# A graph-attention and hypergraph layer over 64 pairs of graphs: another order of the instructions in the software pipeline, and another plan for the preparation of the weights

## The chip, the cores and the metric

One core of one Trainium2 chip. The metric is the device time of the whole program in microseconds (us), as the median of several executions. The engines are called as the profile calls them: PE is TensorE, DVE is VectorE, ACT is ScalarE, POOL is GpSimd, SP is SyncE, which only issues DMA transfers here. I take each engine to work through its own instructions in the order of the program; in the profile of the kernel before, VectorE starts the same 87 instructions in the same order in 57 of the 63 stretches from the nodes of one pair to those of the next.

## The reference, cut to what matters

128 graphs of 128 nodes with 512 features each, fp32. Two layers, each with a residual and a normalisation behind it:

```python
# layer 0: graph attention, 8 heads of 64 features
feats   = einsum('bnf,hfu->bhnu', X, W)                # "pf" below
dense   = leaky_relu(e_self[:, None] + e_neigh[None])  # scores, 128 x 128 per head
dense   = dense + NEG_BIG * (1 - A)                    # mask
att     = softmax(dense)                               # exponentials e, sums
out     = relu(att @ feats + b)                        # "pav"
x       = layernorm(x + out)
# layer 1: two hypergraph convolutions, R = D^-1 H B^-1 H^T from the graph's adjacency
h = relu(R @ (x @ W1.T) + b1)                          # R first: "pz", then "ph"; 1024 wide
h = layer_norm(h) * gamma + beta
y = R @ (h @ W2.T) + b2                                # "py", then "pq"
x = layernorm(x + (y + x))
```

## The kernel before

The kernel takes two graphs (a pair) at a time. Each of the three large products (pf, ph, py) is computed as seven half-size products that gather in three PSUM banks X, Y and W, with sums of operands and of results on the other engines. These seven follow each other on TensorE, and the copies of bank X by ScalarE between them belong to the path:

```python
    def chain(kind, lag, times, multiply, w, extra=0):
        def product(p, s, i):
            where, start = {1: ("X", 1), 2: ("Y", 1), 6: ("X", 0), 5: ("W", 1), 7: ("X", 0),
                            4: ("X", 0), 3: ("W", 0)}[i]
            ...
        def copy(p, s, i):
            ...
            nc.scalar.copy(t[:, :n], s[kind, "X"][:, :n])
```

Every function of the pipeline is placed at a lag (in pairs) and a time within a pair. The order of these numbers is the order of the instructions on the engines; they are no waits. Those that the change moves:

```python
    @step(0, 32.7)
    def nodes(p, s):                 # node degrees of the next pair, on VectorE: seven small operations
        ...
            nc.vector.scalar_tensor_tensor(w[:, g, :], a[:, g, :], 0.0, w[:, g, :],
                op0=ALU.not_equal, op1=ALU.mult, accum_out=dd[:, g:g + 1])
        ...
        nc.vector.tensor_scalar(dn, dd, TINY, None, op0=ALU.max)
        ...
    for (g, q), tm, (lag, tl), (lagx, tx), te, tt in (
        ((0, 0), 32.7, (1, 33.4), (1, 34.8), 2.6, 18.1), ((0, 1), 34.0, (1, 35.7), (1, 37.3), 4.6, 18.15),
        ((1, 0), 35.2, (1, 37.9), (2, 2.0), 5.8, 20.0), ((1, 1), 36.4, (1, 39.0), (2, 2.7), 7.9, 20.7),
    ):
        at(1, tm, masked, g, q)         # GpSimd: scores + mask, one quarter of a pair
        at(lag, tl, leaky, g, q)        # ScalarE
        at(lagx, tx, largest, g, q)     # VectorE: maximum per row ("nm")
        at(2, te, exponential, g, q)    # ScalarE
        at(2, tt, e_transpose, g, q)    # VectorE, behind a trip of the exponentials through DRAM
    ...
    for (g, q), t in (((0, 0), 19.4), ((0, 1), 20.0), ((1, 0), 21.2), ((1, 1), 21.8)):
        at(3, t, square, g, q)          # ScalarE: h squared
    for g in range(2):
        for level in range(3):
            at(3, (25.4, 26.7, 27.4)[level] + 3.9 * g, squares, g, level)   # GpSimd: their sums
```

The weights are prepared within the first pairs. `once` lists this work by the pair in which it falls; `shift` moves one stretch of steps:

```python
    once = {
        0: [(11.0, prepare_first, ())],
        1: [(3.7, prepare_first_sums, ()), (26.3, prepare_hidden, ())],
        2: [(9.0, prepare_output, ()), (9.1, prepare_output_sums, ()),
            (41.5, prepare_output_blocks, (slice(0, 4),))],
        3: [(8.9, prepare_output_block_sums, ())],       # on GpSimd
    }
```

## Time and profile before

| | before |
|---|---|
| time, median | 2774.68 us (2773.65 to 2774.87; three executions, 2774.66 with a fourth) |
| first phX product of pair 0, of pair 1 | 99.80 us, 154.78 us |
| period, from pair 1 to pair 62 (61 pairs) | 41.59 us |
| from pair 62's first phX product to the end | 82.2 us |
| TensorE idle in front of pyW, pyX, phX, each time | 0.93, 0.45, 0.41 us |

I use the start of the first phX product (the first of the seven of ph) as the mark of a pair, since it stands once in each pair on TensorE. The idle times are those of the view of waits, which counts from the modelled end of the product before; the prediction counts from starts and adds the cost of restarting (about 0.1 us each after two of them: 1.83 us for 1.735 and 1.89 for 1.785), and so comes to 2.47 us per pair where these three come to 1.79.

The chain of work that ended last, by engine:

```profile
PE 37%; POOL 34%; DVE 14%; ACT 8%; issue 5%; DMA 1%; SPq 0%; POOLq 0%; DVEq 0%
```

TensorE is busy for 93% of the span, and still the path to the end runs through it for 37% only: in each pair the path leaves TensorE for GpSimd, VectorE and ScalarE and comes back at a hole. What the nodes cost on VectorE in the timeline (start, duration, instruction):

```profile
1019.34 0.28 DVE L305 SCALAR_TENSOR_TENSOR w<-a,w 128x128 f32<-128x128 f32 x1
...
1019.55 1.35 DVE L305 SCALAR_TENSOR_TENSOR w<-a,w 128x128 f32<-128x128 f32 x1
...
1020.94 1.12 DVE L310 TENSOR_SCALAR dn<-dd 128x2 f32<-128x2 f32 x1
```

The same operation on the same shape takes 0.28 and 1.35 us, and one on 128 by 2 elements takes 1.12 us. The long ones run beside the masks on GpSimd (three in a row, 1018.13 to 1022.03 us). Over the whole profile the one on 128 by 2 elements (dn) took 1.11 to 1.12 us in the 62 pairs in which it began while a mask ran, and 0.17 us in the two others.

### The profile page before, as it was taken

To read this page: it belongs to the slowest core of one execution; us is meant where nothing else is said; L and a number is where in the kernel's file an instruction comes from. 1 tells how busy PE (TensorE), PEld (TensorE's weight loads), DVE (VectorE), ACT (ScalarE), POOL (GpSimd) and SP (SyncE) were. 2 spreads that over 40 slices of the span, in tenths; PEclk is the share of its full clock that TensorE was granted. 3 is DMA by queue.
4 is the path that set the end of the run, shared out by engine and by line. 5 is a ranking of instruction groups with operands and counts; after the bars stand their busy time and mean duration, and the time that the engine had idled before them with its cause. 6 is when DMAs were issued, how large, how long until landed. Compare 5 with 4: busy or idle time off the path is not lost.

```text
span 2773.7 us, 48838 instructions
## 1 busy us (share of the span) xinstructions
PE 2576.7 (93%) x16608; PEld 2305.7 (83%) x16608; DVE 2049.4 (74%) x4584; ACT 1533.7 (55%) x4421; POOL 1785.0 (64%) x1813
## 2 busy tenths in 40 slices
PE   3599999999999999999999999999999999999997
PEld 2588888888888888888888888888888888888886
DVE  4577777777777777777777777777777777777764
ACT  2365565565565565565555555555565565555562
POOL 2566666666666666666666666666666666666664
PEclk9799999999999999999999999999999999999998
DMA  5444444444444444444444444444444444444430
GB/s 152 107 124 127 122 124 127 122 124 126 122 124 126 122 124 126 122 124 126 122 124 127 122 123 127 122 122 128 122 123 128 122 123 127 122 122 128 123 109 29
DMA packets 334348, 337.73 MB, mean 122 GB/s; under 512 B 99858, under 2 KB 266770, under 8 KB 334100
## 3 DMA queue, kind: packets, MB, share of 16 engines
q1 hardware_dynamic: 330404, 333.56, 42.6%
q8 instruction: 132, 2.16, 0.3%
q10 hardware_dynamic: 3696, 1.06, 0.2%
q14 instruction: 116, 0.95, 0.1%
HBM read 233.32 MB, written 101.19 MB: 121 GB/s over the span
## 4 chain that ended last, share of the span: by engine, by line
PE 37%; POOL 34%; DVE 14%; ACT 8%; issue 5%; DMA 1%; SPq 0%; POOLq 0%; DVEq 0%
PE phX L678 17%; POOL sq L729 12%; POOL hS L400 10%; PE phW L678 8%; POOL y L576 7%; PE phY L678 4%; PE pq L799 4%; DVE w L305 3%; ACT nb L492 3%; POOL nb L485 3%; ACT h L708 3%; DVE sh L614 3%; DVE dn L310 2%; PE pfX L418 2%; POOL rsa L599 2%
## 5 line engine op out<-in xcount | busy, mean ns | idle before, releaser
L492 ACT ACTIVATE nb<-nb,ft 128x128 f32<-128x128 f32 x1024 | 327.6, 395 | 285.4 <-POOL nb L485 206.0
L678 PEld LDWEIGHTS phX<-zS,w_sb 128*128 128x128 f32 x3072 | 366.2, 193 | 41.2 <-issue 30.4
L678 PE MATMUL phX<-zS,w_sb 128*128 128x128 f32 x3072 | 377.6, 276 | 10.5 <-POOL w_sb L257 7.9
L729 POOL TENSOR_TENSOR sq<-sq 128x512 f32<-128x512 f32 (+2 forms) x384 | 334.1, 870 | 20.1
L485 POOL TENSOR_TENSOR nb<-nb,neg 128x512 f32<-128x512 f32 x256 | 330.2, 1310 | 15.5 <-DMA nb<-rd 15.5
L289 ACT COPY py<-pyX 128x257 f32<-128x257 f32 (+1 forms) x192 | 70.3, 366 | 471.0 <-PE pyX L418 471.0
L506 ACT ACTIVATE nb<-nb,nm 128x128 f32<-128x128 f32 x1024 | 320.8, 394 | 1.8 <-DVE nm L498 1.8
L599 POOL TENSOR_TENSOR rso<-veo,mhalf 128x2 f32<-128x2 f32 x64 | 44.8, 700 | 406.4 <-DVE veo L597 406.4
L418 PE MATMUL pyW<-w_sb,hS 128*128 128x256 f32 x1024 | 249.7, 386 | 56.5 <-DVE y L761 56.5
L418 PE MATMUL pyX<-w_sb,h 128*128 128x257 f32 (+1 forms) x1024 | 251.6, 388 | 28.4 <-ACT py L289 28.1
L418 PEld LDWEIGHTS pyW<-w_sb,hS 128*128 128x128 f32 x1024 | 189.9, 190 | 105.8 <-DVE y L761 81.0
L708 ACT ACTIVATE h<-h,b_sb 128x128 f32<-128x128 f32 x768 | 244.6, 391 | 60.1 <-DVE h L693 60.1
L400 POOL TENSOR_TENSOR hS<-h 128x512 f32<-128x512 f32 x128 | 160.5, 1275 | 179.1 <-ACT h L708 179.1
L552 PEld LDWEIGHTS pav<-ft,eT 128*128 128x128 f32 x2048 | 252.8, 195 | 22.2 <-issue 11.6
L552 PE MATMUL pav<-ft,eT 128*128 128x65 f32 x2048 | 247.2, 275 | 13.4 <-DVE eT L527 13.4
L418 PE MATMUL pyX<-w_sb,hS 128*128 128x257 f32 (+1 forms) x1024 | 243.7, 380 | 2.5 <-POOL hS L400 2.5
L693 DVE TENSOR_TENSOR h<-ph,phW 128x512 f32<-128x512 f32 x128 | 88.0, 688 | 203.8 <-ACT ph L289 138.2
L418 PEld LDWEIGHTS pyX<-w_sb,h 128*128 128x128 f32 x1024 | 185.2, 191 | 55.2 <-ACT py L289 33.8
L418 PEld LDWEIGHTS pyX<-w_sb,hS 128*128 128x128 f32 x1024 | 194.0, 189 | 31.3 <-POOL hS L400 2.9
L576 POOL TENSOR_TENSOR y<-y,b_bc 128x512 f32<-128x512 f32 x128 | 190.4, 1487 | 30.8 <-DVE y L567 30.8
L527 DVE STREAM_TRANSPOSE eT<-eb 128x512 f32<-128x512 f32 x256 | 165.4, 685 | 10.6 <-DMA eb<-ed 10.6
L498 DVE TENSOR_REDUCE nm<-nb 128x4 f32<-128x512 f32 x256 | 168.4, 677 | 6.6 <-ACT nb L492 6.5
(125 smaller groups left out, 5843.5 us busy)
## 6 DMA issues: line engine op xcount, KB each, us to landing
nb<-rd SPq DMA_DIRECT2D x128, 512.0 KB
ed<-nb SPq DMA_DIRECT2D x128, 512.0 KB
eb<-ed SPq DMA_DIRECT2D x512, 128.0 KB
xb<-in_x_dram SPq DMA_DIRECT2D x256, 128.0 KB
x<-in_x_dram SPq DMA_DIRECT2D x64, 512.0 KB
out_dram<-o SPq DMA_DIRECT2D x64, 512.0 KB
a<-in_adj_dram SPq DMA_DIRECT2D x64, 128.0 KB
w<-in_adj_dram SPq DMA_DIRECT2D x128, 64.0 KB
```

Of the source, the lines that this page charges most:

```text
L400: engine.tensor_tensor(t[:, i], in0, in1, op=op)
L418: nc.tensor.matmul(to[:, :n], lhs[:, k, :], rhs[:, k, :n], start=bool(start) and k == 0, stop=(k == nk - 1), skip_group_check=True,)
L485: nc.gpsimd.tensor_tensor(t, t, neg[:, :, None, :].to_broadcast([P, NB, HH, B]), op=ALU.add)
L492: nc.scalar.activation(t, t, AF.Prelu, bias=s["ft"][:, g, h, 0:1], alpha=SLOPE)
L498: nc.vector.tensor_reduce(s["nm"][:, g, hs], scores(s, g, hs).rearrange("p b h j -> p h b j"), AX.XY, ALU.max, negate=True,)
L506: nc.scalar.activation(t, t, AF.Exp, bias=s["nm"][:, g, h:h + 1])
L527: nc.vector.transpose(s["eT"][:, g, hs, :].rearrange("p h (b i) -> p h b i", b=NB), s["eb", g][:, :, hs, :].rearrange("p b h j -> p h b j"),)
L552: nc.tensor.matmul(t[:, h * (U + 1):(h + 1) * (U + 1)], s["eT"][:, g, q * HH + h, :], s["ft"][:, g, q * HH + h, 2:], start=True, stop=True,)
L576: nc.gpsimd.tensor_tensor(s["y"][:, g, :], s["y"][:, g, :], b0_bc, op=ALU.add)
L678: nc.tensor.matmul(to[:, m * N:(m + 1) * N], w[:, k, m * P:(m + 1) * P], rhs[:, k, :], start=bool(start) and m == 0 and k == 0, stop=(k == ...
L708: nc.scalar.activation(dst[:, k, :], src[:, k, :], AF.Relu, bias=b1_sb[:, c:c + 1])
L729: nc.gpsimd.tensor_tensor(t[:, :n, :], t[:, :n, :], t[:, n:2 * n, :], op=ALU.add)
```

## The change

No arithmetic of the loop is added or removed. In the loop: the nodes go from the late place 32.7 to 11.0; masks, squares and their sums come earlier; the last leaky step goes behind the copies of zT; and the transpose of the score rows (pr), with which the load nb for the masks begins, comes half a pav earlier. In the preparation: one list of global times in place of the list by pairs, the third weight's sums on VectorE instead of GpSimd, the first weight in four transfers of rows by fours instead of sixteen by 32 (with a matching layout of the transposed x), and the first pair's exponentials transposed on TensorE instead of through DRAM. Cut to its core:

```diff
-    @step(0, 32.7)
+    @step(0, 11.0)
     def nodes(p, s):
...
-    @step(1, 25.95)
+    @step(1, 24.95)
     def transpose_scores(p, s):
...
-        ((0, 0), 32.7, (1, 33.4), (1, 34.8), 2.6, 18.1), ((0, 1), 34.0, (1, 35.7), (1, 37.3), 4.6, 18.15),
-        ((1, 0), 35.2, (1, 37.9), (2, 2.0), 5.8, 20.0), ((1, 1), 36.4, (1, 39.0), (2, 2.7), 7.9, 20.7),
+        ((0, 0), 31.0, (1, 32.5), (1, 34.8), 2.7, 18.1), ((0, 1), 33.0, (1, 35.4), (1, 37.3), 4.6, 18.15),
+        ((1, 0), 34.2, (1, 38.0), (2, 2.0), 7.8, 21.5), ((1, 1), 35.4, (2, 6.0), (2, 7.3), 7.9, 21.55),
...
-    at(3, 9.2, relu, 0, 0)
+    at(3, 11.5, relu, 0, 0)
-    for (g, q), t in (((0, 0), 19.4), ((0, 1), 20.0), ((1, 0), 21.2), ((1, 1), 21.8)):
+    for (g, q), t in (((0, 0), 13.5), ((0, 1), 15.9), ((1, 0), 19.4), ((1, 1), 21.2)):
         at(3, t, square, g, q)
-            at(3, (25.4, 26.7, 27.4)[level] + 3.9 * g, squares, g, level)
+            at(3, ((17.0, 17.1, 17.2), (26.0, 28.5, 28.6))[g][level], squares, g, level)
...
-        rows = w0.rearrange("(b k f) c -> b f k c", b=NB, k=KF)
-        for b in range(NB):
-            nc.sync.dma_start(raw[b * B:(b + 1) * B],
-                rows[b][:, i * KF // 2:(i + 1) * KF // 2, j * QU:(j + 1) * QU])
+        nc.sync.dma_start(raw, w0.rearrange("(p k) c -> p k c", k=KF)
+            [:, i * KF // 2:(i + 1) * KF // 2, j * QU:(j + 1) * QU])
...
-            s["xb"][:, g * NB:(g + 1) * NB].rearrange("p b (k f) -> p k b f", k=KF),
+            s["xb"][:, g * NB:(g + 1) * NB].rearrange("p b (f k) -> p k b f", k=KF),
...
+    def e_transpose_first(p, s):     # 16 nc.tensor.transpose, 4 nc.scalar.copy; pair 0 alone
...
-    once = { ... }
+    T = 39.2
+    todo = [
+        (11.1, prepare_first, (0,)), (12.0, prepare_first, (1,)), (13.0, prepare_first_sums, ()),
+        (65.0, prepare_output, ()), (71.4, prepare_output_sums, ()), (73.7, prepare_hidden, (0,)),
+        (75.6, prepare_hidden, (1,)), (77.5, prepare_hidden, (2,)), (77.6, prepare_hidden, (3,)),
+        (82.0, prepare_output_blocks, ()), (83.0, prepare_output_block_sums, ()),   # now on VectorE
+    ]
+    def shift(p, lag, time): ...     # moves some steps of pairs 0 and 1
+    for p in range(PAIRS):
+        ...
+            todo.append(((p + lag) * T + time + shift(p, lag, time), on_pair, (fn, p)))
+    todo.append((2 * T + 2.1, on_pair, (e_transpose_first, 0)))
```

More of the change, by code (lines that the diff above doesn't have):

```diff
@@ L130 @@
     w0_blocks = []
-    for dst, i, j in ((w0_sb[:, 0], 0, 0), (w0_12, 0, 1), (w0_sb[:, 1], 1, 0), (w0_sb[:, 2], 1, 1)):
+    for dst, i, j in ((w0_sb[:, 0], 0, 0), (w0_sb[:, 1], 1, 0), (w0_12, 0, 1), (w0_sb[:, 2], 1, 1)):
         raw = work.tile([P, KF // 2, QU], F32, tag=("eT", "nb", "sq", "hS")[2 * i + j], name=f"w0_raw{i}{j}")
-        rows = w0.rearrange("(b k f) c -> b f k c", b=NB, k=KF)
-        for b in range(NB):
-            nc.sync.dma_start(
-                raw[b * B:(b + 1) * B],
-                rows[b][:, i * KF // 2:(i + 1) * KF // 2, j * QU:(j + 1) * QU],
-            )
+        nc.sync.dma_start(
+            raw, w0.rearrange("(p k) c -> p k c", k=KF)
+            [:, i * KF // 2:(i + 1) * KF // 2, j * QU:(j + 1) * QU],
+        )
+        if (i, j) == (1, 0):
+            load_blocks(0)
         w0_blocks.append((dst, raw.rearrange("p k (h u) -> p k h u", h=HH), j))
@@ L147 @@
     an_bc = spread(a_neigh, F, "an_bc")
-    load_blocks(0)
     load(1)
@@ L157 @@
         nc.scalar.dma_start(t, ap.rearrange("(k p) -> p k", p=P))
-    w1_sb = const.tile([P, 7, KF // 2, HALF], F32, name="w1_sb")
     staged = work.tile([P, 2, DH], F32, tag="h", name="staged")
-    w1_21 = staged[:, 0, :].rearrange("p (k c) -> p k c", k=KF // 2)
-    for dst, i, j in ((w1_sb[:, 0], 0, 0), (w1_21, 0, 1), (w1_sb[:, 1], 1, 0), (w1_sb[:, 2], 1, 1)):
-        block(dst, w1t, i, j, F // 2, HALF)
     w2_sb = const.tile([P, 7, KH // 2, QU + 1], F32, name="w2_sb")
@@ L171 @@
         block(dst, w2t, i, j, DH // 2, QU)
+    w1_sb = const.tile([P, 7, KF // 2, HALF], F32, name="w1_sb")
+    w1_21 = staged[:, 0, :].rearrange("p (k c) -> p k c", k=KF // 2)
+    for dst, i, j in ((w1_sb[:, 0], 0, 0), (w1_21, 0, 1), (w1_sb[:, 1], 1, 0), (w1_sb[:, 2], 1, 1)):
+        block(dst, w1t, i, j, F // 2, HALF)
     ident = const.tile([P, P], F32, name="ident")
@@ L192, in second_sums, with prepare_first @@
         eng.tensor_tensor(t4, b21, t2, op=ALU.subtract)
-    def prepare_first():
-        for n, (dst, raw, j) in enumerate(w0_blocks):
+    def prepare_first(half):
+        for n, (dst, raw, j) in list(enumerate(w0_blocks))[2 * half:2 * half + 2]:
             nc.scalar.copy(dst[:, :, :, 2:], raw)
@@ L207, in prepare_first_sums, with prepare_hidden @@
         second_sums(nc.vector, [w0_sb[:, i] for i in range(7)], w0_12)
-    def prepare_hidden():
+    def prepare_hidden(i):
         a11, a12, a22, s1, s2, s3, s4 = (w1_sb[:, i] for i in range(7))
-        nc.vector.tensor_tensor(s1, w1_21, a22, op=ALU.add)
-        nc.vector.tensor_tensor(s2, s1, a11, op=ALU.subtract)
-        nc.vector.tensor_tensor(s3, a11, w1_21, op=ALU.subtract)
-        nc.vector.tensor_tensor(s4, a12, s2, op=ALU.subtract)
+        dst, in0, in1, op = (
+            (s1, w1_21, a22, ALU.add), (s2, s1, a11, ALU.subtract), (s3, a11, w1_21, ALU.subtract),
+            (s4, a12, s2, ALU.subtract),
+        )[i]
+        nc.vector.tensor_tensor(dst, in0, in1, op=op)
     gbs = const.tile([P, KH, 2], F32, name="gbs")
@@ L242, in prepare_output_sums, with prepare_output_blocks @@
         made["gw"] = gw
-    def prepare_output_blocks(some):
+    def prepare_output_blocks():
         gw = made["gw"]
-        for blk, i, j in w2_blocks[some]:
+        for blk, i, j in w2_blocks:
             for k in range(KH // 2):
@@ L254, in prepare_output_block_sums @@
     def prepare_output_block_sums():
-        second_sums(nc.gpsimd, [w2_sb[:, i, :, :QU] for i in range(7)], w2_12)
+        second_sums(nc.vector, [w2_sb[:, i, :, :QU] for i in range(7)], w2_12)
         for i in (0, 1, 5):
@@ L260, with step, at @@
     steps = []
-    def step(lag, time):
+    def step(lag, time, skip_first=False):
         def keep(fn):
-            steps.append((time, len(steps), lag, fn))
+            steps.append((lag, time, fn, skip_first))
             return fn
         return keep
-    def at(lag, time, fn, *args):
-        step(lag, time)(lambda p, s: fn(p, s, *args))
+    def at(lag, time, fn, *args, skip_first=False):
+        step(lag, time, skip_first)(lambda p, s: fn(p, s, *args))
     def chain(kind, lag, times, multiply, w, extra=0):
@@ L453, in transpose_scores, with blocked @@
         )
-    @step(1, 26.2)
+    def blocked(p, t):
+        dims = "(h b j) -> {}b h j" if p == 0 else "(b h j) -> {}b h j"
+        if len(t.shape) == 2:
+            dims = "p " + dims.format("p ")
+        return t.rearrange(dims.format(""), b=NB, h=H)
+    @step(1, 25.4)
     def spread_rows(p, s):
@@ L462, in spread_rows, with scores @@
             nc.sync.dma_start(
-                rd[g].rearrange("b h j -> h b j"),
+                blocked(p, rd[g].rearrange("b h j -> (b h j)")).rearrange("b h j -> h b j"),
                 rows[g * H:(g + 1) * H].rearrange("h (b j) -> h b j", b=NB),
             )
-    @step(1, 28.0)
+    @step(1, 27.0)
     def neighbours(p, s):
-        s["nb"] = work.tile([P, 2 * NB, H, B], F32, tag="nb", name=f"nb_{p}")
+        s["nb"] = work.tile([P, 2, H * N], F32, tag="nb", name=f"nb_{p}")
         for g in range(2):
             nc.sync.dma_start(
-                s["nb"][:, g * NB:(g + 1) * NB].rearrange("p b h j -> p (b h j)"),
+                s["nb"][:, g, :],
                 s["rd"][g].rearrange("b h j -> (b h j)").partition_broadcast(P),
             )
-    def scores(s, g, hs):
-        return s["nb"][:, g * NB:(g + 1) * NB, hs, :]
+    def scores(p, s, g, hs):
+        return blocked(p, s["nb"][:, g, :])[:, :, hs, :]
     def masked(p, s, g, q):
-        t = scores(s, g, slice(q * HH, (q + 1) * HH))
+        t = scores(p, s, g, slice(q * HH, (q + 1) * HH))
         neg = s["neg"][:, g].rearrange("p (b j) -> p b j", b=NB)
@@ L490, in leaky @@
         for h in range(q * HH, (q + 1) * HH):
-            t = scores(s, g, h)
+            t = scores(p, s, g, h)
             nc.scalar.activation(t, t, AF.Prelu, bias=s["ft"][:, g, h, 0:1], alpha=SLOPE)
@@ L498, in largest @@
         nc.vector.tensor_reduce(
-            s["nm"][:, g, hs], scores(s, g, hs).rearrange("p b h j -> p h b j"), AX.XY,
+            s["nm"][:, g, hs], scores(p, s, g, hs).rearrange("p b h j -> p h b j"), AX.XY,
             ALU.max, negate=True,
@@ L504, in exponential @@
         for h in range(q * HH, (q + 1) * HH):
-            t = scores(s, g, h)
+            t = scores(p, s, g, h)
             nc.scalar.activation(t, t, AF.Exp, bias=s["nm"][:, g, h:h + 1])
@@ L510, in e_write @@
         nc.sync.dma_start(
-            s["ed", g], s["nb"][:, g * NB:(g + 1) * NB].rearrange("p b h j -> p b (h j)")
+            s["ed", g], s["nb"][:, g, :].rearrange("p (b x) -> p b x", b=NB)
         )
@@ L530, in e_transpose @@
         )
+    def e_transpose_first(p, s):
+        s["eT"] = work.tile([P, 2, H, N], F32, tag="eT", name=f"eT_{p}")
+        for g in range(2):
+            for q in range(2):
+                t = bank(f"pet_{g}{q}")
+                for h in range(HH):
+                    n = (q * HH + h) * N
+                    nc.tensor.transpose(
+                        t[:, h * N:(h + 1) * N], s["nb"][:, g, n:n + N], ident
+                    )
+                nc.scalar.copy(
+                    s["eT"][:, g, q * HH:(q + 1) * HH, :].rearrange("p h n -> p (h n)"), t
+                )
     for (g, q), tm, (lag, tl), (lagx, tx), te, tt in (
-        ((0, 0), 32.7, (1, 33.4), (1, 34.8), 2.6, 18.1), ((0, 1), 34.0, (1, 35.7), (1, 37.3), 4.6, 18.15),
-        ((1, 0), 35.2, (1, 37.9), (2, 2.0), 5.8, 20.0), ((1, 1), 36.4, (1, 39.0), (2, 2.7), 7.9, 20.7),
+        ((0, 0), 31.0, (1, 32.5), (1, 34.8), 2.7, 18.1), ((0, 1), 33.0, (1, 35.4), (1, 37.3), 4.6, 18.15),
+        ((1, 0), 34.2, (1, 38.0), (2, 2.0), 7.8, 21.5), ((1, 1), 35.4, (2, 6.0), (2, 7.3), 7.9, 21.55),
     ):
@@ L539, with attend @@
         at(2, te, exponential, g, q)
-        at(2, tt, e_transpose, g, q)
+        at(2, tt, e_transpose, g, q, skip_first=True)
     for g in range(2):
-        at(2, (6.2, 9.2)[g], e_write, g)
-        at(2, (10.0, 13.0)[g], e_read, g)
-    def attend(p, s, g):
-        for q in range(2):
-            t = s["pav", g, q] = bank(f"pav_{p}_{g}{q}")
-            for h in range(HH):
-                nc.tensor.matmul(
-                    t[:, h * (U + 1):(h + 1) * (U + 1)], s["eT"][:, g, q * HH + h, :],
-                    s["ft"][:, g, q * HH + h, 2:], start=True, stop=True,
-                )
-    at(2, 20.65, attend, 0)
-    at(2, 24.2, attend, 1)
+        at(2, (6.2, 10.9)[g], e_write, g, skip_first=True)
+        at(2, (10.0, 14.9)[g], e_read, g, skip_first=True)
+    def attend(p, s, g, q):
+        t = s["pav", g, q] = bank(f"pav_{p}_{g}{q}")
+        for h in range(HH):
+            nc.tensor.matmul(
+                t[:, h * (U + 1):(h + 1) * (U + 1)], s["eT"][:, g, q * HH + h, :],
+                s["ft"][:, g, q * HH + h, 2:], start=True, stop=True,
+            )
+    for (g, q), t in (((0, 0), 20.65), ((0, 1), 20.7), ((1, 0), 24.2), ((1, 1), 25.0)):
+        at(2, t, attend, g, q)
     def attended(p, s, g):
@@ L737, in h_sums @@
                    nc.gpsimd, "hS")
-    at(3, 20.3, h_sums, 0)
-    at(3, 21.6, h_sums, 1)
-    at(3, 19.0, h_sums, 2)
-    at(3, 22.8, h_sums, 3)
+    at(3, 20.9, h_sums, 0)
+    at(3, 22.2, h_sums, 1)
+    at(3, 19.6, h_sums, 2)
+    at(3, 23.4, h_sums, 3)
     def weigh(s, i, to, start):
@@ L823, in o_norm @@
         nc.sync.dma_start(out[2 * p:2 * p + 2].rearrange("g n f -> n g f"), s["o"])
-    steps.sort(key=lambda e: e[:2])
-    last = max(lag for _, _, lag, _ in steps)
-    once = {
-        0: [(11.0, prepare_first, ())],
-        1: [(3.7, prepare_first_sums, ()), (26.3, prepare_hidden, ())],
-        2: [(9.0, prepare_output, ()), (9.1, prepare_output_sums, ()),
-            (41.5, prepare_output_blocks, (slice(0, 4),))],
-        3: [(8.9, prepare_output_block_sums, ())],
-    }
-    def shift(t, lag, time):
-        return -17.0 if t == 2 and lag == 1 and time < 27.0 else 0.0
@@ L840 @@
-    with tc.manual_schedule():
-        for t in range(PAIRS + last):
-            todo = list(once.get(t, ()))
-            if 1 < t < PAIRS:
-                load(t)
-            if 0 < t < PAIRS:
-                todo.append((19.0, load_blocks, (t,)))
-            for time, _, lag, fn in steps:
-                if 0 <= t - lag < PAIRS:
-                    todo.append((time + shift(t, lag, time), fn, (t - lag, st[t - lag])))
-            for _, fn, args in sorted(todo, key=lambda e: e[0]):
-                fn(*args)
-            st.pop(t - last, None)
+    T = 39.2
@@ new lines, with on_pair, shift @@
+    todo = [
[4 more added lines that the diff above has]
+    ]
+    def on_pair(fn, p):
+        fn(p, st[p])
+    def shift(p, lag, time):
+        if p == 0:
+            if lag == 0:
+                return 2.5 if time < 20.0 else 0.0
+            if lag == 1 and 4.0 < time < 10.0:
+                return -T + (6.8 if time < 6.0 else 8.0)
+            if lag == 2 and time < 8.5:
+                return -0.8 * time
+        if p == 1 and lag == 1:
+            if time < 3.0:
+                return -3.0
+            return -17.5 if time < 10.0 else -13.0 if time < 12.0 else -23.1 if time < 26.0 else 0.0
+        return 0.0
@@ new lines @@
+    for p in range(PAIRS):
+        if p > 1:
+            todo.append((p * T, load, (p,)))
+        if p:
+            todo.append((p * T + 19.0, load_blocks, (p,)))
+        for lag, time, fn, skip in steps:
+            if p or not skip:
+                todo.append(((p + lag) * T + time + shift(p, lag, time), on_pair, (fn, p)))
+    todo.append((2 * T + 2.1, on_pair, (e_transpose_first, 0)))
+    with tc.manual_schedule():
+        for _, fn, args in sorted(todo, key=lambda e: e[0]):
+            fn(*args)
```

## The prediction

> **What bounds the kernel now.** I began with the page's busy shares and its 40 slices, then read TensorE's timeline over one pair of graphs, then the waits, then the same window on the other engines, then the first 155 us.
>
> ```profile
> PE 2576.7 (93%) x16608; PEld 2305.7 (83%) x16608; DVE 2049.4 (74%) x4584; ACT 1533.7 (55%) x4421; POOL 1785.0 (64%) x1813
> PE   3599999999999999999999999999999999999997
> PEclk9799999999999999999999999999999999999998
> ```
>
> TensorE is busy at over 0.9 in every slice but the first two and the last; nothing else is above 74%. The 64 pairs (two graphs each) run as a software pipeline. By the start of the first phX product, pair 0 begins at 99.80 us, pair 1 at 154.78, pair 61 at 2651.30, pair 62 at 2691.49. So the span is 154.78 (ramp) + 60 x 41.61 + 40.19 + 82.2 (tail). A cut per pair counts sixty times, so the question is what of 41.6 us is not TensorE work. TensorE's timeline from the end of one pair to the next (start, duration, instruction, idle before it and its releaser):
>
> ```profile
> 1017.89 1.89 PE L418 MATMUL pyX<-w_sb,hS 128*128 128x256 f32 x8
> 1019.62 0.61 PE L378 MATMUL pd<-hDT,hB 128*128 128x128 f32 x4
> 1020.06 0.50 PE L772 MATMUL pm<-mean,sq 128*128 128x1 f32 x4
> 1021.02 2.00 PE L418 MATMUL pyX<-w_sb,h 128*128 128x256 f32 x8 [0.45 <-ACT py L289]
> 1023.95 2.00 PE L418 MATMUL pyW<-w_sb,hS 128*128 128x256 f32 x8 [0.93 <-DVE y L761]
> 1025.78 1.95 PE L643 MATMUL pz<-R,y 128*128 128x128 f32 x16
> 1027.57 0.38 PE L328 MATMUL pa<-ident,hD 128*128 128x128 f32 x2
> 1028.35 2.05 PE L678 MATMUL phX<-zT,w_sb 128*128 128x128 f32 x16 [0.40 <-ACT zT L655]
> ```
>
> Three holes repeat; the rest of the period is back to back. Ends of matmuls are modelled, so I use starts. pm needs 4 x 0.11, so the pyX product could start at 1020.50: lost 0.52. It occupies 1.735 (as 1017.89 to 1019.62), so pyW could start at 1022.76: lost 1.19. pa needs 0.22, so phX could start at 1027.79: lost 0.56. Restarting costs about 0.1 after the last two (1.83 for 1.735, 1.89 for 1.785). Sum 2.47: a dense pair is 41.61 - 2.47 = **39.14 us**. (The new plan's constant T = 39.2 agrees.)
>
> Why they wait shows on the other engines in the same window:
>
> ```profile
> 1022.88 0.68 DVE L498 TENSOR_REDUCE nm<-nb 128x4 f32<-128x512 f32 x1
> 1023.48 0.41 DVE L761 TENSOR_TENSOR y<-py,pyW 128x256 f32<-128x256 f32 x1
> ...
> 1019.43 1.28 ACT L492 ACTIVATE nb<-nb,ft 128x128 f32<-128x128 f32 x4 [2.66 <-DMA a<-in_adj_dram]
> 1020.62 0.35 ACT L289 COPY py<-pyX 128x256 f32<-128x256 f32 x1
> ...
> 1026.55 1.28 ACT L492 ACTIVATE nb<-nb,ft 128x128 f32<-128x128 f32 x4 [1.29 <-POOL nb L485]
> 1027.74 1.04 ACT L655 COPY zT<-pz 128x512 f32<-128x512 f32 x2
> ```
>
> The three copies or sums TensorE waits for are late because their in-order engine has other work in front. The py copy stands behind a leaky step that waited for GpSimd's mask (started 1018.13, after rsa). The y sum stands behind the nodes group, DVE 1019.34 to 1022.97. The zT copies stand behind the fourth leaky step, held by the fourth mask, itself behind rsh.
>
> [...] dn<-dd on 128x2 takes 0.17 us at 19.95 with GpSimd idle and 1.12 us at 1020.94 beside the masks. [...] pz takes 3.48 us at 96.27 after idling, 1.95 in the loop; windows at 42 to 54 us show 0.50. [...] 368 GB/s for the weights at 30 us, 188 to 197 for xb and ab at 35 to 37 us, at full engine share.
>
> **The change part by part, in the loop.** Comparing the instruction orders, no steady-state instruction is added or removed; all is order. I place times from phX = 0, with durations from before.
> - Mask (0,0) now precedes rsa on GpSimd, and the first graph's three square sums (2.6) moved ahead of hS, into idle time. GpSimd: squares 15.3 to 17.9, hS to 23.1 (before 22.3; wanted by TensorE at 27.6), remaining sums and biases to 28.4, mask to 29.9 if nb has landed. pr is issued half a pav earlier, so nb's DMA starts about 0.85 sooner; its traffic began at 26.9 and its first half lands near 28.5. Leaky (0,0) is then 30.0 to 31.3, the product ends near 33.0, and the py copy is on time: **0.52** gone.
> - Nodes moved from DVE 1019 to 1023 into the wait before h_sum (2.13 idle). The stretch there becomes: nm (1,1) 5.05 to 5.7, o to 7.5, hB to 8.0, nodes 1.6 (as at 19.41 to 21.03, GpSimd idle) to 9.6; h_sum is released at 9.85. Fits by 0.25. The y sum then runs at 33.5, wanted by 35.4: **1.3** gone.
> - Leaky (1,1) moved behind zT and ph: the copies run as pz ends: **0.66** gone.
> - Squares moved on ScalarE to before pf copies: relu, square, relu, square end at 15.3; pf's copy is due at 15.4. Tight, perhaps 0.1 to 0.3 some time. The second graph's e write starts 1.3 later; read lands near 16.5, its transpose is due at 19.8.
>
> So I expect 39.2 per pair: 60 x 2.41 = **145 us**; the 61-62 interval loses two of the holes, 40.19 to 38.9 (**1.3**). The tail gets 0.4 longer, the square sums now stand before the last hS (2746.5), on which TensorE waits at 2750.39.
>
> **The ramp.** Before:
>
> ```profile
> PE pav L552 <- DVE eT L527: 11.1, 1, 11.1
> PE pz L643 <- ACT y L620: 8.8, 1, 8.8
> PE phX L678 <- POOL w_sb L257: 7.9, 1, 7.9
> PE phX L678 <- POOL zS L666: 2.6, 1, 2.6
> ```
>
> Sixteen w0 transfers become four (11.8 us of queue becomes about 2), so features start earlier, but the first scores' rows still follow all weight loads, ab of pair 1 and its edges on DVE. That load is bandwidth: it ended at 38.4 with some 6 us of slack; I put rows at 34 (36.5 before), masks at 38 (44.7), exponentials done near 57 (62). The round trip of exponentials through DRAM (62.1 to the last eT at 82.2) becomes 16 transposes and four ScalarE copies of 0.57: eT at 60. But DVE now does the w2 blocks (16, 5.6 us) and their sums (4.8), about 52 to 63, and nodes to 64 before it may divide by the sums, so y ends near 67 (87.15). From there 9.1 us to pz as before (87.15 to 96.27) and 3.5: first phX near 79 (99.80). The 7.9 and 2.6 us waits go, with cold clock beside them: pair 0 to 1 in 41 instead of 54.98. Second phX at 120 (154.78): **35 us**, plus or minus 8.
>
> Sum: 120 + 60 x 39.2 + 38.9 + 82.6 = 2593.5; 2.5 added for waits not seen: **2596**.
>
> **Rivals.** (a) *VectorE or ScalarE becomes the bound.* The moved nodes or nm's wait for the late leaky step delays h_sum, relus and the pf copy. For: 0.25 and 0.1 us of room. Against: both engines are idle 20% and more. At 0.4 us per pair: 2620; at a full 1 us, 2656. (b) *nb's transfer takes the place of the mask wait*: mask (0,0) now stands in front of rsa, so a late nb delays sh, first_output and pz. Speaks for it: x and a share the queue; against: traffic for nb started at 26.9 and carried 1 MB by 30.6. Half a microsecond late is still hidden. (c) *The ramp gives less*: rows held by DMA, or TensorE cold longer: 10 to 15 us worse. (d) *Loop gain hidden*, only the ramp counts: 2740; I see no mechanism, since TensorE's holes are themselves on the path.
>
> **Range and chances.** 60 pairs at 39.14 to 39.6 span 27 us, the ramp adds 8 either way: 2581 to 2624. Slower than 2719 would need 90% of the loop gain and part of the ramp gone: faster 0.97.
>
> **What would show it.** Right: phX to phX 39.2; no idle before pyX, pyW, phX; TensorE back to back; second phX near 120; no eb transfer for pair 0; DVE w_sb blocks before the first rden. Wrong: a new repeating hole before pfX (copy late), pr (ft late) or pz (rsa behind nb), or a period above 39.8; a granted clock below 1.00 from denser work; a second phX past 130.

## The result, and the profile after

The changed kernel takes **2601.47 us** (median of 4 runs, 2601.11 to 2603.63), the kernel before 2774.66 us in the same rounds. The ratio is 0.9378, with a 95% interval of 0.9362 to 0.9394. Ratios here and below are the mean time of one kernel's runs over that of the other's of the same rounds, so they are not quite the ratios of the medians quoted. A second measurement, with the experiments, gave 2601.63 us and 0.9375.

From the page of the changed kernel: busy shares, granted clock in 40 slices, and the chain that ended last, by engine:

```profile
PE 2530.2 (97%) x16624; PEld 2298.1 (88%) x16624; DVE 2027.5 (78%) x4584; ACT 1555.9 (60%) x4425; POOL 1720.3 (66%) x1809
...
PEclk9899999999999999999999999999999999999998
...
PE 96%; DVE 1%; DMA 1%; issue 1%; POOL 0%; ACT 0%; SPq 0%; POOLq 0%; DVEq 0%; ACTq 0%
```

The path now lies on TensorE for 96% of the span, where it was 37%. The granted clock did not fall with the denser work (0.992 on average, 0.987 before). TensorE's timeline over the seam between two pairs shows why the path stays on it:

```profile
1025.18 0.50 PE L792 MATMUL pm<-mean,sq 128*128 128x1 f32 x4
1025.55 1.98 PE L419 MATMUL pyX<-w_sb,h 128*128 128x256 f32 x8
1027.36 1.89 PE L419 MATMUL pyW<-w_sb,hS 128*128 128x256 f32 x8
1029.10 1.95 PE L663 MATMUL pz<-R,y 128*128 128x128 f32 x16
1030.88 0.38 PE L329 MATMUL pa<-ident,hD 128*128 128x128 f32 x2
1031.10 1.95 PE L698 MATMUL phX<-zT,w_sb 128*128 128x128 f32 x16
```

None of these lines has a bracket any more, that is, no idle time in front. The view of TensorE's waits between 200 and 2480 us is empty. The nodes on VectorE, at their new place:

```profile
1000.13 0.28 DVE L306 SCALAR_TENSOR_TENSOR w<-a,w 128x128 f32<-128x128 f32 x1
...
1000.34 0.28 DVE L306 SCALAR_TENSOR_TENSOR w<-a,w 128x128 f32<-128x128 f32 x1
...
1000.66 0.17 DVE L311 TENSOR_SCALAR dn<-dd 128x2 f32<-128x2 f32 x1
```

They cost 1.6 us here (1000.13 to 1001.74, the end of the last of them) instead of 3.6 us (1019.34 to about 1022.9), and GpSimd runs no mask beside them. In all 64 pairs dn took 0.17 us here, with no operation of GpSimd beside it; b_nodes below, which moves the nodes alone, has the same mean.

Where the time went, by the marks of the two profiles:

| stretch | before | after | difference | predicted |
|---|---|---|---|---|
| start to first phX of pair 1 | 154.78 | 131.26 | -23.5 | -35 |
| pair 1 to pair 62 | 2536.71 | 2386.30 | -150.4 | -146 |
| pair 62 to the end | 82.2 | 84.3 | +2.1 | +0.4 |

### The profile page after: what moved, and what is told of

It reads as the page before. It is cut to its first block, busy times and chain, and to the rows that moved or that the text cites. A ratio compares the mean times of both kernels' runs of the same rounds, so it can differ in the third digit from the quotient of the medians.

```text
span 2601.9 us, 48690 instructions
## 1 busy us (share of the span) xinstructions
PE 2530.2 (97%) x16624; PEld 2298.1 (88%) x16624; DVE 2027.5 (78%) x4584; ACT 1555.9 (60%) x4425; POOL 1720.3 (66%) x1809
## 4 chain that ended last, share of the span: by engine, by line
PE 96%; DVE 1%; DMA 1%; issue 1%; POOL 0%; ACT 0%; SPq 0%; POOLq 0%; DVEq 0%; ACTq 0%
PE pyX L419 17%; PE phX L698 17%; PE pfX L419 9%; PE phW L698 9%; PE pyW L419 8%; PE pav L572 8%; PE pz L663 4%; PE phY L698 4%; PE pfW L419 4%; PE pyY L419 4%; PE pq L819 4%; PE pfY L419 2%; PE pd L379 1%; PE pm L792 1%; PE pa L329 1%
## 5 line engine op out<-in xcount | busy, mean ns | idle before, releaser
L492 POOL TENSOR_TENSOR nb<-nb,neg 128x512 f32<-128x512 f32 x256 | 320.1, 1271 | 75.7 <-DMA nb<-rd 75.7
L749 POOL TENSOR_TENSOR sq<-sq 128x512 f32<-128x512 f32 (+2 forms) x384 | 321.6, 837 | 36.3 <-ACT sq L738 21.1
L419 PE MATMUL pyW<-w_sb,hS 128*128 128x256 f32 x1024 | 242.3, 378 | 0.0
L686 POOL TENSOR_TENSOR zS<-zT 128x256 f32<-128x256 f32 x128 | 93.5, 730 | 210.3 <-ACT zT L675 210.3
L505 DVE TENSOR_REDUCE nm<-nb 128x4 f32<-128x512 f32 x256 | 174.2, 681 | 23.3 <-ACT nb L499 22.9
L290 ACT COPY ph<-phX 128x512 f32<-128x512 f32 x192 | 112.4, 585 | 88.9 <-PE phX L698 88.9
```

Source lines behind the costliest of these rows:

```text
L419: nc.tensor.matmul(to[:, :n], lhs[:, k, :], rhs[:, k, :n], start=bool(start) and k == 0, stop=(k == nk - 1), skip_group_check=True,)
L492: nc.gpsimd.tensor_tensor(t, t, neg[:, :, None, :].to_broadcast([P, NB, HH, B]), op=ALU.add)
L505: nc.vector.tensor_reduce(s["nm"][:, g, hs], scores(p, s, g, hs).rearrange("p b h j -> p h b j"), AX.XY, ALU.max, negate=True,)
L749: nc.gpsimd.tensor_tensor(t[:, :n, :], t[:, :n, :], t[:, n:2 * n, :], op=ALU.add)
```

## The experiments

Twelve kernels were run, all correct. Those called u_ undo a part of the change, those called b_ do one part alone in the kernel before, those called x_ change something further.

### Undoing the loop's parts

u_nodes and u_leaky act from the third pair on, so that the preparation stays as changed. The edit of u_gpsimd, also a part of u_loop, has no such condition and acts on all pairs, although the expectations say otherwise. The start hardly shows it: pair 1's first phX comes at 131.91 and 129.64 us, where the changed kernel has 131.26 and 129.55 in two executions. The nodes back (u_nodes), the last leaky step back (u_leaky), GpSimd's order back (u_gpsimd; the squares on ScalarE and the early pr stay), and all three (u_loop):

```diff
 # u_nodes, in shift()
+        if p > 1 and lag == 0 and time == 11.0:
+            return 21.7
 # u_leaky, in shift()
+        if p > 1 and lag == 2 and time == 6.0:
+            return 33.0 - T
+        if p > 1 and lag == 2 and time == 7.3:
+            return -4.6
 # u_gpsimd
-        ((0, 0), 31.0, (1, 32.5), ...), ((0, 1), 33.0, (1, 35.4), ...),
-        ((1, 0), 34.2, ...), ((1, 1), 35.4, ...),
+        ((0, 0), 32.7, (1, 33.4), ...), ((0, 1), 34.0, (1, 35.7), ...),
+        ((1, 0), 35.2, ...), ((1, 1), 36.4, ...),
-            at(3, ((17.0, 17.1, 17.2), (26.0, 28.5, 28.6))[g][level], squares, g, level)
+            at(3, (25.4, 26.7, 27.4)[level] + 3.9 * g, squares, g, level)
```

Expected of u_nodes:

> The changed kernel with one part undone: from the third pair on the nodes (node minus mean on VectorE and GpSimd) stand late in the pair again, as before. Theory: the mask-and-column sum y on VectorE again ends behind them, so TensorE again stands idle once per pair in front of the pyW products, by 1.2 to 1.3 us: some 62 pairs by 1.2 us, about +75 us, 2676 us (2660 to 2690). Rival: the copy of py on ScalarE, or nothing, governs that place, and the kernel stays under 2622 us. The profile should show waits of TensorE in front of pyW and none in front of pyX and phX.

Expected of u_leaky:

> The changed kernel with one part undone: from the third pair on the leaky step of the last score tile and the maximum behind it stand at their old, late places. Theory: ScalarE copies zT later by some 0.8 us, and TensorE stands idle in front of phX by 0.45 to 0.65 us per pair again: +27 to +40 us, 2630 to 2640 us. Rival: the masks come so early now that the leaky step costs ScalarE no waiting, and the kernel stays within 10 us of 2602 us.

Expected of u_gpsimd:

> The changed kernel with one part undone: masks, squares and the first two leaky steps (GpSimd's share of the new order) at their old times from the third pair on. Theory: ScalarE gets the last masked scores late and copies py late, so TensorE stands idle in front of pyX by about 0.5 us per pair, and not in front of pyW: about +32 us, 2634 us (2620 to 2650). Rivals: nothing at all, as the nodes out of the way leave VectorE and GpSimd slack (2602 us); or more, over 60 us, if the fourth mask also delays the copy of zT.

Expected of u_loop:

> The three undone parts (nodes; leaky step; masks and squares) together from the third pair on, the preparation and the first pairs kept as changed. Theory: all of the loop's gain goes, 2.47 us per pair in 61 pairs, about +150 us, 2750 us (2740 to 2760), and about 25 us of gain, that of the preparation, stay against the kernel before. If the parts act one by one, +150 us is about the sum of the three single runs; if they stand in for each other, the single runs add up to clearly less (each hole needs only one cause) or more.

Measured. The last three columns are TensorE's mean wait per pair in front of that product; the period is from pair 1 to pair 62 in the profile.

| kernel | median us | ratio to before | period us | pyW | pyX | phX |
|---|---|---|---|---|---|---|
| before | 2774.66 | 1 | 41.59 | 0.93 | 0.45 | 0.41 |
| changed | 2601.47 | 0.9378 | 39.12 | 0 | 0 | 0 |
| u_nodes | 2709.23 | 0.9764 | 40.80 | 1.41 | 0 | 0 |
| u_leaky | 2632.37 | 0.9486 | 39.59 | 0 | 0 | 0.20 |
| u_gpsimd | 2636.91 | 0.9499 | 39.67 | 0 | 0.39 | 0 |
| u_loop | 2749.48 | 0.9903 | 41.51 | 0.93 | 0.38 | 0.41 |

TensorE's waits between 200 and 2480 us in u_nodes, u_leaky and u_gpsimd (in total, times, longest):

```profile
PE pyW L419 <- DVE y L781: 79.2, 56, 2.4
```

```profile
PE phX L698 <- ACT zT L675: 11.7, 58, 0.2
```

```profile
PE pyX L419 <- ACT py L290: 22.6, 58, 0.7
```

Each undone part brings back one hole, the one that was expected of it, and no other. u_leaky brings back half of its hole by this view, 0.20 us of 0.41 (0.45 to 0.65 was expected, counted from starts; the period grew by 0.47). The times of u_leaky and u_gpsimd came out as expected (2630 to 2640, 2634), and u_loop too (2749.5 for 2750): all of the loop's gain lies in the order of these steps, and about 26 us of the change's gain remain, that of the preparation.

One was wrong. **u_nodes** lost 107.8 us by the medians, not 75, and its hole in front of pyW is 1.41 us where the kernel before has 0.93. And the singles add up to too much: 1.68 + 0.47 + 0.55 = 2.70 us per pair by the periods, against 2.39 for all three together. Something is counted twice. The timelines gave a theory: with late nodes the sum y in front of pyW started 8.6 us after the sum behind pyY in u_nodes, 8.7 in u_loop and 8.8 in the kernel before (medians of 60 pairs). That stretch of VectorE's work hardly depends on what TensorE does meanwhile. If TensorE doesn't wait in front of pyX, it comes to pyW earlier and waits there for longer. The next two kernels test this from the other side.

### One part alone in the kernel before

b_nodes is the kernel before with `@step(0, 11.0)` on the nodes and nothing else. b_gpsimd is the kernel before with the change's order of masks, first two leaky steps, one relu, squares, their sums and the operand sums of h (delayed by 0.6 to make room), with nodes, last leaky step and pr late:

```diff
 # b_nodes
-    @step(0, 32.7)
+    @step(0, 11.0)
 # b_gpsimd
-        ((0, 0), 32.7, (1, 33.4), ...), ((0, 1), 34.0, (1, 35.7), ...),
-        ((1, 0), 35.2, ...), ((1, 1), 36.4, ...),
+        ((0, 0), 31.0, (1, 32.5), ...), ((0, 1), 33.0, (1, 35.4), ...),
+        ((1, 0), 34.2, ...), ((1, 1), 35.4, ...),
-    at(3, 9.2, relu, 0, 0)
+    at(3, 11.5, relu, 0, 0)
-    for (g, q), t in (((0, 0), 19.4), ((0, 1), 20.0), ((1, 0), 21.2), ((1, 1), 21.8)):
+    for (g, q), t in (((0, 0), 13.5), ((0, 1), 15.9), ((1, 0), 19.4), ((1, 1), 21.2)):
-            at(3, (25.4, 26.7, 27.4)[level] + 3.9 * g, squares, g, level)
+            at(3, ((17.0, 17.1, 17.2), (26.0, 28.5, 28.6))[g][level], squares, g, level)
```

Expected of b_nodes:

> The kernel before with one part of the change alone: the nodes at their new, early place. Theory: the hole in front of pyW, 1.2 us per pair, goes, and those in front of pyX and phX stay: -75 us, about 2700 us (2685 to 2715). Rival: y or the copy of py waits for something else just as long (masks on GpSimd, squares), and the time stays above 2750 us.

Expected of b_gpsimd:

> The kernel before with the new order of masks, squares, their ScalarE operations and the first two leaky steps alone; nodes and the last leaky step stay late. Theory, formed from the runs so far: the sum y in front of pyW ends a fixed 8.4 to 8.8 us after the sum behind pyY, whatever TensorE does in between, so with late nodes the idle time in front of pyX is only moved in front of pyW when it is taken away: pyX without a wait, pyW waiting about 1.4 to 1.8 us instead of 0.93, and only 5 to 20 us of gain, 2755 to 2770 us. Rival: the three holes are independent, and the kernel gains the 33 to 35 us that the same part cost when it was undone alone, 2740 us.

| kernel | median us | before, same rounds | ratio | period us | pyW | pyX | phX |
|---|---|---|---|---|---|---|---|
| b_nodes | 2688.58 | 2773.32 | 0.9693 | 40.20 | 0 | 0.45 | 0.20 |
| b_gpsimd | 2815.41 | 2775.07 | 1.0147 | 42.12 | 2.20 | 0 | 0 |

**b_nodes** gained 84.7 us, somewhat more than expected. The hole in front of pyW is gone, that in front of pyX stayed as it was, and half of that in front of phX went too. The fourth mask stands on GpSimd behind rsh (the scale of the second normalisation), which is computed from the sum y; with y earlier, that mask is earlier and so is the leaky step in front of the zT copies. That the wait went from 0.41 to 0.20 is measured; that this is the way is read from the order on the engines.

**b_gpsimd** was expected to gain 5 to 20 us, or by the rival 33 to 35, and it lost 40. What was expected of the holes did happen, and more: those in front of pyX and phX are gone, and all the waiting stands in front of pyW. But that hole is 2.20 us, not 1.4 to 1.8. Two causes show in its profile. First, on VectorE:

```profile
1071.74 1.20 DVE L597 TENSOR_SCALAR vea<-mva 128x2 f32<-128x2 f32 x1
```

and on GpSimd the first mask, now in front of rsa (the scale of the first normalisation):

```profile
1071.65 1.27 POOL L485 TENSOR_TENSOR nb<-nb,neg 128x512 f32<-128x512 f32 x1 [1.44 <-DMA nb<-rd]
```

vea, the input of rsa, stands on the way to y. Its mean is 0.17 us in the kernel before and 0.93 us in b_gpsimd. It started while GpSimd worked on the mask (until 1072.92) and ended with it. The stretch from the sum behind pyY to y became 9.58 us in this pair, 9.43 in the median, instead of 8.8. My theory had it fixed, and that was wrong: the early mask lengthened it. The mask in turn waited for its load nb, and the change's early pr, which b_gpsimd leaves out, is what brings that load earlier. In u_nodes, which has the early masks, the early pr and late nodes, pr starts 23.1 us after phX and the mask 29.1; in b_gpsimd 24.0 and 29.9. vea takes 0.54 us there, the stretch 8.6 and the hole 1.41. So the extra 0.8 us of this hole goes with the late pr; no run moved pr alone. Second, TensorE's timeline over two such holes, one pair apart, and busy times with the granted clock (the 1.00 and 0.68 behind the five engines' times) of the stretches behind them:

```profile
1037.77 2.00 PE L418 MATMUL pyW<-w_sb,hS 128*128 128x256 f32 x8 [2.14 <-DVE y L761]
...
1079.50 2.93 PE L418 MATMUL pyW<-w_sb,hS 128*128 128x256 f32 x8 [2.33 <-DVE y L761]
```

```profile
1037.70:1041.60 3.90, 3.83 (x26) 3.61 (x27) 2.87 (x10) 1.94 (x7) 1.08 (x2) 1.00 0.00 0
...
1079.50:1084.80 5.30, 5.30 (x25) 4.79 (x26) 3.34 (x10) 1.66 (x5) 1.08 (x2) 0.68 0.03 7
```

After some of these holes TensorE goes on at a lower granted clock (0.68 over the 5.30 us from pyW's start in the second pair shown, 1.00 in the first). In 21 of the 60 pairs that the trace has whole, the time from pyW's start to the next phX is 5.48 to 5.50 us instead of 3.83 to 3.84. That is 1.65 x 21 / 60 = 0.58 us per pair. Without it the period would be 42.12 - 0.58 = 41.54 us, the same as before (41.59). So in this kernel the longer stretch took back what the closed holes gave, and the lower clock makes it a loss. Which pairs it hits does not follow from the length of the hole: the 21 have 2.22 us on average, the others 2.19. None of the 60 holes of 0.93 us in the kernel before is followed by it, and none of 59 holes of 1.03 to 1.80 us in u_nodes; the one of 2.42 us there is.

The granted clock, which the trace file holds as a list of stretches, shows which ones are hit. The distances between the starts of its stretches are whole multiples of 3.413 us, all 13 in the kernel before and all 9 in the changed kernel, each to within 0.002 us. I call these points, 3.41 us apart, the grid of an execution. In b_gpsimd it goes through the drops (the first three drops of this loop at 237.31, 363.60 and 489.90 us, each 37 steps behind the one before), and each drop in this loop lasts one step of it, as here (PEclk 0.50):

```profile
1080.40:1083.81 3.41, 3.41 (x14) 2.98 (x13) 1.59 (x4) 0.17 (x1) 0.81 (x2) 0.50 0.00 0
```

In the 21 pairs a grid point comes 0.85 to 1.44 us after the start of pyW; in the 39 others 1.48 to 2.64 us. The two groups do not overlap: of these 60 holes, the 21 that ended at most 1.44 us before a grid point were followed by the lower clock, and the 39 that ended 1.48 us or more before one were not.

The nodes' place carries most of the gain, as the one that shortens VectorE's work between pyY and pyW: that stretch is 5.59 us in the changed kernel, of which 0.47 on average is a wait for the py copy. GpSimd's order (u_gpsimd) is worth about 35 us once the nodes are out of the way. With late nodes it depends on what comes with it: with the early pr in place, it and the leaky step bring 40 us (u_nodes beside u_loop, 40.80 for 41.51 us per pair); in b_gpsimd, without the early pr and with the leaky step late, it loses 40.

### Undoing parts of the preparation

The first pair's exponentials through DRAM again (u_etrans), and the first weight's rows by 32, with the old layout of x (u_w0):

```diff
 # u_etrans
-        dims = "(h b j) -> {}b h j" if p == 0 else "(b h j) -> {}b h j"
+        dims = "(h b j) -> {}b h j" if p < 0 else "(b h j) -> {}b h j"
-            if p or not skip:
+            if True:
-    todo.append((2 * T + 2.1, on_pair, (e_transpose_first, 0)))
 # u_w0
-        nc.sync.dma_start(raw, w0.rearrange("(p k) c -> p k c", k=KF)[...])
+        rows = w0.rearrange("(b k f) c -> b f k c", b=NB, k=KF)
+        for b in range(NB):
+            nc.sync.dma_start(raw[b * B:(b + 1) * B], rows[b][...])
-            s["xb"][:, g * NB:(g + 1) * NB].rearrange("p b (f k) -> p k b f", k=KF),
+            s["xb"][:, g * NB:(g + 1) * NB].rearrange("p b (k f) -> p k b f", k=KF),
```

Expected of u_etrans:

> The changed kernel with the first pair's exponentials transposed through DRAM again instead of on TensorE. Theory: in the preparation the first y is held by VectorE, which is busy with the third weight's blocks and sums until 77.4 us, and the transposed exponentials were there by about 68 us, so most of the transfer's extra time is hidden: +2 to +6 us, about 2606 us. Rival: the whole extra time of a store and a load, 10 to 16 us, stands on the path: 2612 us or more.

Expected of u_w0:

> The changed kernel with the rows of the first weight in the old layout, 32 by 32 blocks in more and smaller transfers, instead of by fours. Theory: the raw transfers of the start come later by a few us, which VectorE's later queue absorbs in part: 0 to +6 us, about 2604 us. Rival: the first weight's landing sets the whole start, and the kernel is slower by 8 us or more.

The marks of the preparation, in us from the start of the profiled execution, for these kernels and those of the next part. "Rows" is the copy of pair 0's score rows on VectorE, with which the scores begin; "rden" is the first division by the sums, with which y begins.

| kernel | median us | ratio | rows | rden | phX of pair 0 | phX of pair 1 |
|---|---|---|---|---|---|---|
| before | 2774.66 | 1 | 36.48 | 82.11 | 99.80 | 154.78 |
| changed | 2601.47 | 0.9378 | 42.99 | 77.39 | 92.59 | 131.26 |
| after_again | 2601.63 | 0.9375 | 42.55 | 75.98 | 91.18 | 129.55 |
| u_etrans | 2608.35 | 0.9406 | 42.10 | 79.49 | 97.97 | 137.13 |
| u_w0 | 2602.38 | 0.9384 | 43.79 | 77.01 | 91.95 | 130.31 |
| x_nodes0 | 2598.40 | 0.9370 | 37.51 | 71.74 | 86.94 | 125.53 |
| x_w2late | 2597.36 | 0.9362 | 42.94 | 68.54 | 83.74 | 123.25 |
| x_both | 2590.81 | 0.9339 | 38.15 | 63.84 | 81.59 | 121.11 |

The period is 39.12 us in all of these but the kernel before. after_again is the changed kernel unchanged, run to see how much its start differs from one execution to the next:

> The changed kernel itself once more, to see how far its start differs from one execution to the next and from one chip to the next: every theory expects 2601 to 2604 us and a ratio of 0.937 to 0.939; the first phX product of pair 1 is expected between 128 and 132 us, since kernels with the same start showed 128.2 to 131.9 us.

It came out as expected. The profiled execution of the first measurement was its slowest, by 2 us; the start differs by 2 to 3 us between executions. A difference of less than that in one profile means nothing here.

**u_etrans** costs 6.9 us by the medians and 5.9 to 7.6 by the mark of pair 1, a little more than expected. The transfer through DRAM itself is hidden: the exponentials were there when VectorE became free, at 76.7 us, from the third weight. What costs is that VectorE then has 2.5 us of transposes to do, and that TensorE, idle for 14.6 us, took 7.09 us for the products pav that take 3.79 in the changed kernel, where the 16 transposes run right ahead of them. (In u_w0 they took 7.09 us behind the transposes too, but there VectorE was still at the third weight.) **u_w0** is 0.9 us slower by the medians and inside the intervals: the layout by fours gains nothing that this measurement can show. It has a price instead that I had not looked for. The transposes of x on VectorE (128x512) take a mean of 1.11 us in the loop of the changed kernel, 0.69 in u_w0 and 0.69 in the kernel before, 0.85 us per pair for the two. VectorE has that to spare, so it costs nothing now.

### Where the preparation's missing gain is

Two theories for why the second phX came at 131.26 and not at 120. The first: the score rows are late, as the queue of SyncE stands still. In the changed kernel the nodes of pair 0 are placed behind all of the first weight's sums on VectorE (27.63 to 29.9 us); the load that reuses their buffer w holds the queue from 22.4 to 28.9, with the adjacency blocks of pair 1 behind it. The second: VectorE prepares the third weight in front of the first y. x_nodes0 moves the nodes between the two halves of the first weight's work, where VectorE was idle. x_w2late moves half of the third weight's blocks and all its sums behind the first y. x_both does both, and sets the squares of the last two pairs' first graphs 8.4 later, for the tail.

```diff
 # x_nodes0, in shift()
-                return 2.5 if time < 20.0 else 0.0
+                return 0.6 if time < 20.0 else 0.0
 # x_w2late, in todo
-        (82.0, prepare_output_blocks, ()), (83.0, prepare_output_block_sums, ()),
+        (82.0, prepare_output_blocks, (slice(0, 2),)), (83.0, prepare_output_ones, ()),
+        (116.0, prepare_output_blocks, (slice(2, 4),)), (119.7, prepare_output_block_sums, ((0, 2),)),
+        (130.0, prepare_output_block_sums, ((1, 3),)),
 # x_both: the two above, and in shift()
+        if p >= PAIRS - 2 and lag == 3 and 17.0 <= time <= 17.2:
+            return 8.4
```

Expected of x_nodes0:

> The changed kernel with the first nodes placed between the two halves of the first weight's sums on VectorE, where it was idle. Theory: the queue of SyncE is no longer held by the store behind them, TensorE's in-order first score products are not held up by hD until 29.9 us, and the adjacency rows arrive earlier: rows at about 37.5 us instead of 43.0, the first phX at 87 us instead of 92.6: -5 to -6 us, about 2596 us. Rival: the adjacency rows are bound by the raw transfers themselves, or VectorE's later blocks take the gain back: 0 to -1 us.

Expected of x_w2late:

> The changed kernel with the third weight's blocks and sums split and moved behind the first y on VectorE. Theory: VectorE's preparation of the third weight until 77.4 us is what holds the first y; without it y ends near 69 us instead of 79.7, bound then by the exponentials' transposes at 68 us, and the first phX comes 7 to 8 us earlier (85 us instead of 92.6): -5 to -8 us, about 2595 us. Rival: the moved work delays pair 1 (h_sum, score steps) and gives the gain back: 0 to -2 us, or slower.

Expected of x_both:

> Both: first nodes early, and the third weight's blocks and sums behind the first y; besides, the squares of the last two pairs' first graphs 8.4 us later, where they don't stand beside the normalisation on VectorE. Theory: the two gains of the start act in sequence (rows early, so exponentials early, so y early), and the tail gives back about 1 us: -12 to -15 us against the changed kernel, about 2588 us. Rival: they share one bound, and the sum is that of the better one, -8 us or less.

First the changed kernel itself. TensorE's waits in its first 160 us, the two long ones:

```profile
PE pa L329 <- DVE hD L316: 29.9, 1, 29.9
PE pz L663 <- ACT y L640: 17.5, 1, 17.5
```

and VectorE's timeline from the rows to the first division:

```profile
42.99 0.26 DVE L467 COPY rows<-pr 16x128 f32<-16x128 f32 x1
...
64.87 1.65 DVE L250 SCALAR_TENSOR_TENSOR w_sb<-w_sb,gb,gw 128x256 f32<-128x256 f32 x4
...
74.72 1.22 DVE L192 TENSOR_TENSOR w_sb<-w_sb 128x1024 f32<-128x1024 f32 x1
...
77.39 0.17 DVE L586 RECIPROCAL rden<-pav 128x4 f32<-128x4 f32 x1
```

The first wait ends with the nodes (hD, their result). pa, its transpose, stands in front of pair 0's features in TensorE's order, so those wait with it. The second is the wait for y: pav was done at 70.6 us, and VectorE came to it at 77.39, after 11 us on the third weight (64.87 to 75.9) and the nodes of a later pair.

Each theory's kernel moved what it named. In **x_nodes0** the rows came 5.5 us earlier, held then only by the arrival of the adjacency of pair 1:

```profile
36.21 0.45 DVE L357 STREAM_TRANSPOSE hT<-ab 128x256 f32<-128x256 f32 x1 [3.03 <-DMA ab<-in_adj_dram]
...
37.51 0.26 DVE L467 COPY rows<-pr 16x128 f32<-16x128 f32 x1
```

and every later mark came 5.6 to 5.7 us earlier than in the first profile of the changed kernel, 4.0 to 4.2 earlier than in the second. In **x_w2late** the rows stayed and the first division came 7.4 to 8.9 us earlier; of this 0.8 is lost between pairs 0 and 1 (39.51 us for 38.67), where the moved work stands now. By the medians the two are worth 3.2 and 4.3 us against the second measurement of the changed kernel. Their marks show 4.0 and 6.3, more than the times do; both are at the edge of what the intervals resolve.

**x_both** takes 2590.81 us, 10.8 us less than the changed kernel and the fastest here; 12 to 15 was expected. The sum of the two gains would have put pair 0's phX near 78. It came at 81.59, and TensorE's timeline says where the rest is:

```profile
61.10 7.09 PE L577 MATMUL pav<-ft,eT 128*128 128x65 f32 x32
```

This took 3.79 us in the changed kernel. The products came earlier but took 3.3 us longer. Two profiles show the granted clock beside such times: 0.50 where pav of pair 0 took 7.06 us (the kernel before), 1.00 where it took 3.79 (the changed kernel). By the profiles, 8.4 us of the gain lie in the start and some 4 in the tail: from pair 62 to the end took 79.9 us, instead of 84.1 in after_again. I had expected 1. In the changed kernel the normalisation of o on VectorE stands beside GpSimd's moved squares and takes 1.9 us for 1.0, the last pairs' transposes come 0.9 later, TensorE waits 3.2 us for them instead of 2.3, and pav behind that wait took 5.63 us in after_again and 3.79 in x_both.

The longer pav in the start goes with where the grid of its execution lies. In front of the 16 transposes TensorE waits 2.07 or 2.08 us in all kernels that have them. In u_leaky, u_gpsimd, u_w0 and x_both the next grid point came 1.04 to 1.78 us after the end of this wait, and pav took 7.09 us; in both executions of the changed kernel, u_nodes, x_nodes0 and x_w2late it came after 2.06 to 3.00 us, and pav took 3.79. (u_loop had 0.53 and 4.04 us.) The two executions of the changed kernel had 2.69 and 2.06 us, so the grid lies differently each time, and x_both's 3.3 us look like chance of the profiled execution.

What stays open: a part of the distance to 120 is not explained by a kernel of its own: even with rows at 37.5 us they are later than the 34 predicted, held by the transfer of the adjacency behind the weights.

## Why the prediction was right or wrong, point by point

- **A dense pair of 39.14 us, from counting starts: right.** The period is 39.12. The prediction took 39.2 and 2.5 us for waits not seen; neither the last 0.1 nor the 2.5 was needed there, and the loop came out 4.6 us better than its terms.
- **Each moved step closes its hole: right, and shown.** The three undone parts bring back one hole each. What the prediction's three separate numbers (0.52, 1.3, 0.66) hide is that they can't be had one by one: b_gpsimd closed two of them and lost time, since all the waiting moved on to pyW and grew there.
- **The nodes fit into the wait before h_sum by 0.25: right, barely.** In the trace they end at 1001.74 and the sum starts at 1001.73; it starts 9.75 us after phX, and 9.85 was predicted. VectorE has no slack left at that place.
- **Rival (a), VectorE or ScalarE becomes the bound: did not happen.** ScalarE's pf copy waits 0.88 us for TensorE and not the other way round.
- **Rival (b), nb's transfer takes the mask's place: the wait is there, and it is hidden.** GpSimd waits 1.20 us on average for that transfer in front of the first mask (75.7 us in 63 waits), and no wait of TensorE follows from it. In b_gpsimd, where pr starts 0.9 us later, the hole at pyW grows.
- **The 61-62 interval of 38.9 us: right** (38.90).
- **The tail gets 0.4 longer: wrong in size**, 2.1. The step "the square sums now stand before the last hS" saw the delay of hS, and missed the normalisation on VectorE, which takes 1.9 us beside the same squares and 1.0 without them in x_both.
- **The ramp, "Second phX at 120 (154.78): 35 us": the step that failed.** It gave 23.5 to 25.2 us (131.26 and 129.55), about the size of rival (c), and beyond the plus or minus 8 given. The sign of being wrong, "a second phX past 130", came in the first profile and was missed by 0.45 us in the second. Two terms of its sum were mis-sized. "I put rows at 34": they came at 43.0, later than before, as the queue stood behind the nodes. And "so y ends near 67": it ended at 79.66. The prediction put the third weight's blocks and sums at "about 52 to 63", beside the exponentials; in VectorE's order they stand behind the last maximum of pair 0's scores, so they began at 64.87 and came on top. x_nodes0 and x_w2late each took away one of these and moved the marks accordingly. The other two terms held: from y to pz 8.9 us (9.1 predicted), and from pair 0 to pair 1 38.67 us (41 predicted), without the waits for GpSimd's sums.
- **The sum.** The prediction's terms gave 2593.5 us. They were off by +11.3 in the ramp, -4.6 in the loop and +1.7 in the tail, together +8.4, which is the 2601.9 us of the profile's span. The time was missed by only 5.5 us (2601.47 for 2596), since the loop's gain over its terms and the 2.5 us added for waits not seen paid for more than half of the ramp. That these errors offset each other is luck.

## What to carry to other kernels

When one engine should be dense, take all of its holes in one period together with the work between them on the other engines: here, with the first of two holes on the same chain removed, the second grew from 0.93 us to 1.41 (u_nodes) and 2.20 (b_gpsimd), and 21 of 60 of the latter were followed by 3.41 us at a granted clock of 0.50. A part cut out of a plan must take along what it leans on: b_gpsimd, with the early masks but not the early pr, lost 40 us. Look at what runs on GpSimd beside each short VectorE operation on the path, as the seven moved out of the masks' company took 1.6 us instead of 3.6. In a preparation, count the in-order queue, not the free time of an engine: work "that fits beside" is only beside if it is placed in front of what waits (the first division came at 77.39 us behind the third weight's work, and at 68.54 in x_w2late, which places a part of that work behind it).
